# Context products in groups of four slot blocks instead of two, with the value work placed later and the mean loads cut in halves

## The chip, the cores and the metric

The kernel runs on one core of a Trainium2 chip. The time is the device time of one execution in microseconds; the median of three runs of the kernel before is 1081.12 us (1079.87 to 1084.78). Under half a percent, some 5 us, a difference can hardly be told from none.

A core has five engines that run side by side, each with a queue of its own that is worked off in order: TensorE (PE, the matmuls), VectorE (DVE), ScalarE (ACT), GpSimd (POOL, here the indirect DMAs) and SyncE (SP, here all other DMAs). They wait for each other through semaphores. Matmul results land in PSUM, all other tiles lie in SBUF.

## The reference

```python
def _L0_cond_ref(x, mask, Wq, Wo):           # x [16, 512, 1024], mask [16, 1024] of 0 and 1
    xt = jnp.transpose(x, (0, 2, 1))          # [16, 1024 tokens, 512 features]
    q = xt @ Wq.T
    qh = q.reshape(B, T, NH, dk).transpose(0, 2, 1, 3)         # 8 heads of 64
    scores = scale * jnp.einsum('bhqd,bhkd->bhqk', qh, qh)     # queries, keys and values are one
    logits = (scores * cmask + (1.0 - cmask) * NEG) * rmask
    attn = jax.nn.softmax(logits, axis=-1)
    ctx = jnp.einsum('bhqk,bhkd->bhqd', attn, qh)
    return jnp.transpose(ctx... @ Wo.T, (0, 2, 1))
x = x + _L0_cond_ref(x, cond_2048, L0_cond_Wq, L0_cond_Wo)
```

A token whose mask is 0 is no key for the others, and its own row of logits is all zero, so that its attention is the plain mean over all 1024 tokens. About half of the tokens are active.

## The kernel before, in words

**The work of one batch.** There are 16 batches. In each, the active tokens (384 to 544 are allowed for) are given "slots" 0 to 543. `index` makes the list of row numbers, `gather` fetches the rows of x by indirect DMA on POOL (four tiles `xa` of 128 rows and one `xt` of 32), `xt` transposes them on PE (line 424) and `xsplit` splits them into two fp16 halves `xh` (ACT, line 384) and `xl` (DVE, line 385). `query` multiplies them with the weights, three fp16 products for each of 4 feature chunks, so 12 matmuls for one of 8 calls (line 447, copy by ACT in line 450); it is called for e = 0 to 3 (pairs of heads) and g = 0, 1 (halves of the slots). `qsplit` splits the queries again (`hl`, DVE), and four DMAs on SP spread them into a tile `xx` from which the scores are computed. These DMAs are issued one step later than `qsplit` (the list `later`). `value` turns the queries of one pair of heads into rows by slot: 8 small matmuls that read `xx` (line 497), an ACT copy `v` (line 500), squares and maxima on DVE. `peaks`, `top` and `bottom` make from the maxima the shift `nm` for the exponentials. `sum_half` sums the loaded features over the tokens on ACT (line 369), for the mean; `load_all` loads them on SP, 512 KB at a time into one of two `xm` buffers (line 374).

**The steps.** The order of emission is written out in `run`. A batch is a list S of 18 steps: for each pair of heads p = 0 to 3 and each slot block i = 0 to 3 of 128 slots one step, and two more steps (i is None) for the tails of 32 slots (line 595). A step (p, i) emits `scores` for head 2p, then filler work, then `scores` for head 2p+1. One `scores` is 4 matmuls (line 620) into a PSUM tile `pss`, of which there are two, and one exponential on ACT (line 624) from it into a tile `p`, of which there are 9. The context of the step is not computed at once: `attend` is put on the list `todo`. At i = 0 and i = 2 what stands there is moved to `ready`, and at i = 1 and i = 3 it is emitted, so that two slot blocks make one group. A group is the context product of line 643 for two slot blocks: 8 float32 matmuls in the program, each two instructions in the trace, into 64 of the 128 columns of the array, the two heads side by side (`k` is 1, then 0). All of a pair's products add up in one PSUM tile `pav`; `attend` with i = 4 adds the tail (line 647) and copies the sum out on ACT (line 651).

**The filler.** The other work of the batch (`m`) is one list of pairs of a cost and a function: the norms and the projection of the batch before (`project`: 12 matmuls of 512 columns, line 727), the transposes, queries and values of the batch after. `fill` emits from it until the summed cost reaches the share that the list `share` grants for this place. In `m` the letters q, v, P_, x, tc, tv, pk, tp, bt stand for query, value, project, xt, tail_copy, value_tail, peaks, top, bottom; o is the batch before, n the batch after. `free` holds the work of certain steps that costs PE nothing, loads and sums among it. The smaller PSUM tiles of the filler (`pm`) share two buffers, so the next but one waits until the engine that reads a tile has done so.

**What orders the engines.** A scheduler of the framework makes each engine's queue from this order of emission; matmuls of a group are kept together and have a raised priority (`behind`, `high_priority`). The queues themselves are in order: an exponential that has to wait holds back every ACT instruction behind it.

Of the kernel before, what the change touches and what calls it, by code (L numbers as in the profile page):

```python
# [10 lines left out]
F32 = mybir.dt.float32  # L11
# [38 lines left out]
class Fast:  # L50
# [320 lines left out]
    def load_all(self, b, c, after=None):  # L371

        t = self.sb([P, T], F32, "xm", 2)
        self.once(self.nc.sync.dma_start(out=t, in_=self.x_nat[b, c * P:(c + 1) * P, :]), after)
        self.st[b]["xm"].append(t)

    def xsplit(self, dst, src, scaled=False):
# [204 lines left out]
    def scores(self, b, p, i):  # L582
# [6 lines left out]
        if i is None:  # L589
            pt = self.ps_s.tile([P, 2, 512], F32, tag="s", name="pss")  # L590
            for a in range(2):
                for g in range(2):
                    for r in range(HG):
                        xx, k = s["xx"][2 * p + r // 2], r % 2
                        self.beat = nc.tensor.matmul(pt[r * CT:(r + 1) * CT, g, :CH], lhsT=xx[:, 2 * k, 512:C],  # L595
                                                     rhs=xx[:, 2 * k + a, g * CH:(g + 1) * CH],
                                                     start=(a == 0), stop=(a == 1)).ins
            t = self.sb([P, C], F32, "p", 9)
            nc.scalar.activation(t.rearrange("p (g c) -> p g c", g=2), pt[:, :, :CH], AF.Exp,
                                 bias=s["nm"][p][:, HG:], scale=SCALE, accum_out=s["zt"][:, p:p + 1])  # L600

            hi = self.sb([P, C], F32R, "c", 4)
            lo = t.bitcast(F32R)
            nc.vector.tensor_copy(hi, t)
            nc.vector.tensor_tensor(lo, t, hi.bitcast(F32), ALU.subtract)

            def spread():
                s["pt"] = self.sb([P, 2, C], F32R, "pt")
                half = slice(0, DK), slice(DK, P)
                for k in range(2):  # L610
                    nc.sync.dma_start(out=s["pt"][half[k], k, :].bitcast(F32), in_=hi[half[k]].bitcast(F32))
                    nc.sync.dma_start(out=s["pt"][half[1 - k], k, :].bitcast(F32), in_=lo[half[k]].bitcast(F32))

            self.later(spread)
            return None
        xx, k = s["xx"][p // 2], p % 2
        pt = self.ps_s.tile([P, 2, 512], F32, tag="s", name="pss")
        for a in range(2):
            for g in range(2):
                self.beat = nc.tensor.matmul(pt[:, g, :CH], lhsT=xx[:, 2 * k, i * P:(i + 1) * P],  # L620
                                             rhs=xx[:, 2 * k + a, g * CH:(g + 1) * CH],
                                             start=(a == 0), stop=(a == 1)).ins
        t = self.sb([P, C], F32, "p", 9)
        self.exp = [nc.scalar.activation(t.rearrange("p (g c) -> p g c", g=2), pt[:, :, :CH], AF.Exp,  # L624
# [4 lines left out]
    def attend(self, b, p, i, ps):  # L629
        nc, s = self.nc, self.st[b]  # L630

        if i == 1:
            s["pav"] = self.ps_av.tile([P, 2, 512], F32, tag="av", name="pav")
        for g in range(2):
            for k in (1, 0) if i < 4 else range(2):
                cols = slice(g * CH, (g + 1) * CH)
                if i < 4:
                    with ExitStack() as st:
                        if self.group_first:
# [3 lines left out]
                        mm = nc.tensor.matmul(s["pav"][k * DK:(k + 1) * DK, g, :CH], lhsT=s["v"][p][:, i, k * DK:(k + 1) * DK],  # L643
                                              rhs=ps[k][:, cols], start=(i == 1), stop=False)
                    self.group_first = self.group_first or mm.ins
# [199 lines left out]
    def run(self, flag):  # L845
# [99 lines left out]
        if True:  # L945
            for b in range(B + 1):
                o, n = b - 1, b + 1
                if b == B:
                    self.last(o, todo)
                    break  # L950
# [14 lines left out]
                if n < B:  # L965
# [5 lines left out]
                    take = [(0, L(self.gather, b + 2, j)) for j in range(5)] if ahead else []  # L971
                    m = sums + x[:2] + (value(b, 3) if b else []) + pk(b, 1) + second + x[2:4] + rows + x[4:]
                    for g in new[0]:
                        m += [(0, L(self.active, *g))]
                    m += q(0, 0) + tp(b, 1) + (q(0, 1) if b else bt(b, 1) + q(0, 1))
                    for g in new[0]:
# [4 lines left out]
                    for g in new[1]:  # L981
                        m += [(0.1, L(self.facts_end, *g))]
                    m += rng[:2] + tc(0) + tail + v(0) + P_(0) + tv(0) + rest + v(1) + P_(1) + (hot if b else []) + rng[2:] + q(2, 0) + (index if b else [])
                    m += pk(n, 0) + q(2, 1) + tp(n, 0) + P_(2) + (take if b else []) + q(3, 0) + v(2) + bt(n, 0)
                    m += q(3, 1) + tc(1) + [(0, L(self.means, n))] + P_(3) + tv(1)
                    if b == 0:
# [19 lines left out]
                if b + 2 < B:  # L1006
                    self.start(b + 2)
                    for c in range(DC):
                        at = 3 * c + (0 if b else 4)
                        free.setdefault(at, []).append(L(self.load_all, b + 2, c, None if b else first_top))  # L1010
                        free.setdefault(at + 4, []).append(L(self.sum_half, b + 2, c))
                if b == 0:
                    for k in range(2 * DC):
                        free.setdefault(1 + k // 3, []).append(L(self.sum_half, 1, k))

                share = [(1.2, 0) if i is None else ((0.95, 0.95), (0.9, 0), (0.45, 0.95), (0.9, 0))[i] for _, i in S]
                unit = sum(c for c, _ in m) / sum(map(sum, share))
# [10 lines left out]
                for st, (p, i) in enumerate(S):  # L1028
# [15 lines left out]

                    if i in (0, 2):
                        ready, todo = todo, []
                    elif i in (1, 3):
                        self.group_first = None
                        for f in ready[1::-1] + ready[2:]:
                            f()  # L1050
                        ready = []
# [158 lines left out]
```

## Time and profile before

| | |
|---|---|
| median of three runs | 1081.12 us |
| the profiled execution | 1081.4 us, of it a span of 1079.7 us from first to last instruction |
| mean granted clock of TensorE | 0.995 |
| PE busy | 1038.1 us, 96% of the span |
| ACT busy | 681.6 us, 63% |
| DVE busy | 745.6 us, 69% |
| exponentials, line 624 | 512, 717 ns each |
| context products, line 643 | 2048 instructions, busy 262.9 us together |
| scores, line 620 | 2048 instructions, busy 317.6 us together |

A group's line in the profile names the line of the kernel, the engine, the operation, the tiles and shapes, the count, then after a bar the busy time and the mean of one in ns, and after a second bar the time that the engine sat idle just before them and what ended it. In a timeline each row has a start and a length in us, and merges equal instructions; since matmuls are pipelined, lengths of neighbours overlap, and the start of the next row tells when the engine went on.

### The profile page before, as it was taken

To read this page: it belongs to the slowest core of one execution; us is meant where nothing else is said; L and a number is where in the kernel's file an instruction comes from. 1 tells how busy PE (TensorE), PEld (TensorE's weight loads), DVE (VectorE), ACT (ScalarE), POOL (GpSimd) and SP (SyncE) were. 2 spreads that over 40 slices of the span, in tenths; PEclk is the share of its full clock that TensorE was granted. 3 is DMA by queue.
4 is the path that set the end of the run, shared out by engine and by line. 5 is a ranking of instruction groups with operands and counts; after the bars stand their busy time and mean duration, and the time that the engine had idled before them with its cause. 6 is when DMAs were issued, how large, how long until landed. Compare 5 with 4: busy or idle time off the path is not lost.

```text
span 1079.7 us, 23837 instructions
## 1 busy us (share of the span) xinstructions
PE 1038.1 (96%) x8626; PEld 690.9 (64%) x8626; DVE 745.6 (69%) x2376; ACT 681.6 (63%) x1722; POOL 303.0 (28%) x303
## 2 busy tenths in 40 slices
PE   6889999999999999999999999999999999999996
PEld 6566667666666666666666666667666665666553
DVE  6687768676675767766785776868667775666553
ACT  5777667666676766666576666666666565665550
POOL 3101022222202223222233323222232331335652
PEclk9999999999999999999999999999999999999999
DMA  6746465556655554656556566554755554565752
GB/s 205 211 126 177 133 175 154 174 150 190 174 141 158 171 173 145 198 176 169 177 147 197 154 186 193 152 171 135 229 176 173 177 149 127 149 182 166 222 175 84
DMA packets 78125, 181.39 MB, mean 168 GB/s; under 512 B 15008, under 2 KB 16800, under 8 KB 78000
## 3 DMA queue, kind: packets, MB, share of 16 engines
q1 hardware_dynamic: 56816, 111.62, 36.6%
q0 software_dynamic: 21184, 68.18, 20.8%
q8 instruction: 70, 1.15, 0.5%
q14 instruction: 55, 0.45, 0.1%
HBM read 92.34 MB, written 33.91 MB: 117 GB/s over the span
## 4 chain that ended last, share of the span: by engine, by line
PE 82%; DMA 7%; DVE 3%; ACT 2%; issue 2%; SPq 2%; POOL 0%; POOLq 0%; ACTq 0%; DVEq 0%
PE pav L643 21%; PE pss L620 19%; PE pm L727 15%; PE pm L447 14%; DMA xx<-hl 6%; PE pm L424 3%; PE pav L647 3%; PE pss L595 2%; PE pm L497 2%; PE pm L680 1%; ACT q L450 1%; SPq L470 1%; ACT p L624 1%; PE pm L520 1%; DMA rb<-rd 1%
## 5 line engine op out<-in xcount | busy, mean ns | idle before, releaser
L624 ACT ACTIVATE p<-pss,nm 128x544 f32<-128x544 f32 x512 | 365.5, 717 | 210.5 <-PE pss L620 203.6
L620 PE MATMUL pss<-xx 128*128 128x272 f16 x2048 | 317.6, 280 | 3.1 <-ACT p L624 2.7
L643 PE MATMUL pav<-p,v 128*64 128x272 f32 x2048 | 262.9, 399 | 0.0
L620 PEld LDWEIGHTS <-xx 128*128 128x128 f16 x2048 | 191.9, 100 | 73.2 <-issue 27.7
L643 PEld LDWEIGHTS pav<-p,v 128*64 128x64 f32 x2048 | 135.6, 136 | 94.3 <-issue 27.1
L811 POOL DMA_INDIRECT y_out<-xa,idx x68 | 70.2, 1032 | 288.6 <-issue 91.5
L447 PE MATMUL pm<-xh,wqh 128*128 128x274 f16 (+1 forms) x512 | 143.3, 280 | 3.3 <-DVE nm L560 1.9
L447 PE MATMUL pm<-xl,wqh 128*128 128x274 f16 (+1 forms) x512 | 142.9, 279 | 0.2 <-DVE xl L385 0.2
L447 PE MATMUL pm<-xh,wql 128*128 128x274 f16 (+1 forms) x512 | 143.0, 279 | 0.0
L339 POOL DMA_INDIRECT xa<-x_in,idx x68 | 69.5, 1023 | 167.1 <-PE pss L620 71.0
L447 PEld LDWEIGHTS <-wqh 128*128 128x128 f16 x1024 | 99.3, 98 | 25.9 <-issue 6.7
L811 POOL DMA_INDIRECT y_out<-xi,idx x60 | 74.0, 1233 | 137.7 <-DVE xi L798 38.3
L624 ACT ACTIVATION_READ_ACCUMULATOR p<-pss,nm 128x1 f32 x512 | 102.6, 200 | 0.0
L450 ACT ACTIVATE q<-pm 128x272 f32<-128x272 f32 (+1 forms) x128 | 50.8, 397 | 81.6 <-PE pm L447 81.6
L727 PE MATMUL pm<-woh,ch 128*128 128x512 f16 x240 | 91.8, 382 | 0.3 <-DVE tmp L523 0.3
L727 PE MATMUL pm<-wol,ch 128*128 128x512 f16 x240 | 91.7, 382 | 0.0
L727 PE MATMUL pm<-woh,cl 128*128 128x512 f16 x240 | 91.5, 381 | 0.0
L732 DVE SCALAR_TENSOR_TENSOR xa<-pm,xa 128x512 f32<-128x512 f32 x60 | 41.4, 690 | 72.4 <-PE pm L727 72.3
L339 POOL DMA_INDIRECT xi<-x_in,idx x60 | 61.3, 1021 | 106.1 <-PE pss L620 49.5
L727 PEld LDWEIGHTS <-ch 128*128 128x128 f16 x480 | 46.7, 98 | 45.6 <-issue 2.2
L369 ACT ACTIVATE xm<-xm 128x1024 f32<-128x1024 f32 (+1 forms) x62 | 62.5, 1009 | 2.3 <-DMA xm<-x_nat_in 2.3
L711 DVE TENSOR_TENSOR c<-c,rb 128x544 f32<-128x544 f32 x64 | 46.1, 720 | 22.4 <-PE pss L620 11.1
(194 smaller groups left out, 1550.0 us busy)
## 6 DMA issues: line engine op xcount, KB each, us to landing
xx<-hl SPq DMA_DIRECT2D x256, 136.0 KB
xm<-x_nat_in SPq DMA_DIRECT2D x56, 512.0 KB
rb<-rd SPq DMA_DIRECT2D x128, 136.0 KB
pt<-c SPq DMA_DIRECT2D x64, 136.0 KB
pt<-p SPq DMA_DIRECT2D x64, 136.0 KB
ub<-ud SPq DMA_DIRECT2D x16, 256.0 KB
xi<-x_nat_in SPq DMA_DIRECT2D x8, 256.0 KB
xa<-x_in,idx POOLq DMA_INDIRECT x68, 4.5
```

Source lines behind the costliest of these rows:

```text
L339: dma = self.nc.gpsimd.indirect_dma_start(out=tile[:n], out_offset=None, in_=self.x, in_offset=bass.IndirectOffsetOnAxis(ap=idx, axis=0))
L369: self.nc.scalar.activation(s["xm"][k], s["xm"][k], AF.Copy, accum_out=s["ms2"][:, k:k + 1])
L424: self.pe = nc.tensor.transpose(pt[:, c, :], x[:n, c * P:(c + 1) * P], self.ident[:n, :n]).ins
L447: self.beat = nc.tensor.matmul(pq, lhsT=w[:, c, e * P:(e + 1) * P], rhs=xx[:, c, cols], start=(k == 0), stop=(k == 3 * DC - 1)).ins
L450: nc.scalar.activation(s["q"][:, e, cols], pq, AF.Copy, scale=1.0 / (SX * SW))
L620: self.beat = nc.tensor.matmul(pt[:, g, :CH], lhsT=xx[:, 2 * k, i * P:(i + 1) * P], rhs=xx[:, 2 * k + a, g * CH:(g + 1) * CH], start=(a == ...
L624: self.exp = [nc.scalar.activation(t.rearrange("p (g c) -> p g c", g=2), pt[:, :, :CH], AF.Exp, bias=s["nm"][p // HG][:, p % HG:p % HG + 1 ...
L643: mm = nc.tensor.matmul(s["pav"][k * DK:(k + 1) * DK, g, :CH], lhsT=s["v"][p][:, i, k * DK:(k + 1) * DK], rhs=ps[k][:, cols], start=(i == ...
L711: self.once(nc.vector.tensor_tensor(c, c, s["rb"][p], ALU.mult), self.beat if p < 3 else None)
L727: nc.tensor.matmul(po[:cols.stop - cols.start], lhsT=a[:, e, cols], rhs=w[:, e, :], start=(e == 0 and k == 0), stop=(e == DC - 1 and k == 2))
L732: self.nc.vector.scalar_tensor_tensor(x, po, 1.0 / (SX * SW), x, ALU.mult, ALU.add)
L811: dma = self.nc.gpsimd.indirect_dma_start(out=self.out, out_offset=bass.IndirectOffsetOnAxis(ap=idx, axis=0), in_=x, in_offset=None)
```

## The change

The context groups become twice as long: `ready` is filled at i = 0 alone and emitted at i = 1, all four slot blocks of the pair of heads before, in the order 3, 2, 1, 0 (and then the tail, where it is there). There are 12 buffers for `p` instead of 9. In `m`, each `value` stands further behind, the peaks of the later heads as well, and the grants in `share` differ. `load_all` becomes two DMAs of 256 KB, the second one a step after the first, and the sum comes three steps after the first half instead of four.

```diff
     def load_all(self, b, c, after=None):
         t = self.sb([P, T], F32, "xm", 2)
-        self.once(self.nc.sync.dma_start(out=t, in_=self.x_nat[b, c * P:(c + 1) * P, :]), after)
+        self.load_part(t, b, c, 0, after)
         self.st[b]["xm"].append(t)
+
+    def load_part(self, t, b, c, k, after=None):
+        cols = slice(k * T // 2, (k + 1) * T // 2)
+        self.once(self.nc.sync.dma_start(out=t[:, cols], in_=self.x_nat[b, c * P:(c + 1) * P, cols]), after)
...
-        t = self.sb([P, C], F32, "p", 9)
+        t = self.sb([P, C], F32, "p", 12)
...
-        if i == 1:
+        if i == 3:
             s["pav"] = self.ps_av.tile([P, 2, 512], F32, tag="av", name="pav")
...
-                                              rhs=ps[k][:, cols], start=(i == 1), stop=False)
+                                              rhs=ps[k][:, cols], start=(i == 3), stop=False)
...
-                    self.last(o, todo)
+                    self.last(o, todo[3::-1] + todo[4:])
...
-                    m = sums + x[:2] + (value(b, 3) if b else []) + pk(b, 1) + second + x[2:4] + rows + x[4:]
+                    m = sums + x[:2] + second + x[2:4] + (value(b, 3) if b else []) + rows + x[4:] + pk(b, 1)
...
-                    m += q(0, 0) + tp(b, 1) + (q(0, 1) if b else bt(b, 1) + q(0, 1))
+                    m += q(0, 0) + (q(0, 1) + tp(b, 1) if b else tp(b, 1) + bt(b, 1) + q(0, 1))
...
-                    m += rng[:2] + tc(0) + tail + v(0) + P_(0) + tv(0) + rest + v(1) + P_(1) + (hot if b else []) + rng[2:] + q(2, 0) + (index if b else [])
-                    m += pk(n, 0) + q(2, 1) + tp(n, 0) + P_(2) + (take if b else []) + q(3, 0) + v(2) + bt(n, 0)
-                    m += q(3, 1) + tc(1) + [(0, L(self.means, n))] + P_(3) + tv(1)
+                    m += rng[:2] + tc(0) + tail + P_(0) + v(0) + tv(0) + rest + P_(1) + (hot if b else []) + rng[2:] + q(2, 0) + v(1) + (index if b else [])
+                    m += q(2, 1) + pk(n, 0) + P_(2) + (take if b else []) + tp(n, 0) + q(3, 0) + bt(n, 0)
+                    m += q(3, 1) + v(2) + tc(1) + [(0, L(self.means, n))] + P_(3) + tv(1)
...
-                        free.setdefault(at + 4, []).append(L(self.sum_half, b + 2, c))
+                        free.setdefault(at + 1, []).append(lambda n=b + 2, c=c: self.load_part(self.st[n]["xm"][c], n, c, 1))
+                        free.setdefault(at + 3, []).append(L(self.sum_half, b + 2, c))
...
-                share = [(1.2, 0) if i is None else ((0.95, 0.95), (0.9, 0), (0.45, 0.95), (0.9, 0))[i] for _, i in S]
+                share = [(1.2, 0) if i is None else ((1.0, 0.6), (0.1, 0.5), (0.9, 1.0), (0.9, 0.9))[i] for _, i in S]
...
-                    if i in (0, 2):
+                    if i == 0:
                         ready, todo = todo, []
-                    elif i in (1, 3):
+                    elif i == 1:
                         self.group_first = None
-                        for f in ready[1::-1] + ready[2:]:
+                        for f in ready[3::-1] + ready[4:]:
                             f()
```

More of the change, by code (lines that the diff above doesn't have):

```diff
@@ L622, in scores @@
                                              start=(a == 0), stop=(a == 1)).ins
-        t = self.sb([P, C], F32, "p", 9)
+        t = self.sb([P, C], F32, "p", 12)
         self.exp = [nc.scalar.activation(t.rearrange("p (g c) -> p g c", g=2), pt[:, :, :CH], AF.Exp,
```

## The prediction

> **What bounds the kernel now.** First the busy times, the slices and the chain of the page.
>
> ```profile
> PE 1038.1 (96%) x8626; PEld 690.9 (64%) x8626; DVE 745.6 (69%) x2376; ACT 681.6 (63%) x1722; POOL 303.0 (28%) x303
> PE   6889999999999999999999999999999999999996
> PEclk9999999999999999999999999999999999999999
> PE 82%; DMA 7%; DVE 3%; ACT 2%; issue 2%; SPq 2%; POOL 0%; POOLq 0%; ACTq 0%; DVEq 0%
> ```
>
> PE is full from slice 4 on, at a clock that no change can raise, and 82% of the chain is PE. So only two things give time: fewer microseconds of PE work, or fewer gaps in it. For the work I looked at the context group around 508 us in the PE timeline, in windows so narrow that rows are not merged.
>
> ```profile
> 507.99 0.28 PE L620 MATMUL pss<-xx 128*128 128x272 f16 x1
> 508.20 0.45 PE L643 MATMUL pav<-p,v 128*64 128x272 f32 x2
> ...
> 509.62 0.40 PE L643 MATMUL pav<-p,v 128*64 128x272 f32 x2
> 509.85 0.40 PE L643 MATMUL pav<-p,v 128*64 128x272 f32 x2
> ...
> 510.18 0.33 PE L680 MATMUL pm<-ident,rcol 128*128 128x128 f32 x1
> ```
>
> Pairs of context matmuls (two heads side by side) follow each other every 0.23 us. But the first starts 0.21 us after the last score, where scores follow each other after 0.116, and the next work starts 0.33 us after the last pair instead of 0.23: about 0.1 us lost going in and 0.1 coming out. The trace's starts give 0.05 more between the first pair and the second (0.28). So a group carries 0.247 us beside its work, and there are 4 x 2 x 16 = 128 groups.
>
> For the gaps I read the waits of PE and a place where they stand.
>
> ```profile
> L497 PE MATMUL pm<-two,xx 128*128 128x64 f16 x480 | 26.6, 193 | 13.1 <-DMA xx<-hl 11.4 <-ACT qt L508 1.3
> L620 PE MATMUL pss<-xx 128*128 128x272 f16 x2048 | 317.6, 280 | 3.1 <-ACT p L624 2.7 <-DMA xx<-hl 0.2
> ```
>
> ```profile
> 503.32 0.19 PE L497 MATMUL pm<-two,xx 128*128 128x64 f16 x1 [1.32 <-ACT qt L508]
> ...
> 505.27 0.38 PE L497 MATMUL pm<-two,xx 128*128 128x64 f16 x7 [0.86 <-DMA xx<-hl]
> ```
>
> The value matmuls are the one group that PE stands still for: 13.1 us, nearly all for the spread of the queries that has not landed. Scores wait 3.1 us for the exponentials in the whole run, so ACT is no bound.
>
> **The change, part by part.** The sum is made against the profiled execution, 1081.4 us, which is 0.3 us above the median of 1081.12.
>
> *Groups of four.* The instructions are the same 2048. The built program's order shows 64 unbroken groups of 16 program matmuls where there were 128 of 8, so 64 entries and exits go: 64 x 0.247 = 15.8 us, all on PE and so on the path. A rule here: the Trainium skill (TensorEngine Tiling (Array Packing), Tiling Modes) says that a change of tiling mode drains the array, and its page TensorE: Matmul & The Clock Gate (Single matmul latency) puts the fixed part of a lone warm matmul at some 166 ns. An estimate from that page, a full drain in and one out, is 64 x 2 x 0.166 = 21 us. The row's 0.1 us each way is this shape itself, so I take 15.8.
>
> *Later values.* In the built order `value` 0 and 1 each have a projection (12 x 0.215 = 2.6 us) or more put ahead of them, `value` 2 a query (12 x 0.116 = 1.4 us) and more. The longest wait for the spread is 1.9 us, so 2.6 us cover it. The last batch keeps its order; its two waits, 0.65 and 0.93 us, stay. That is 13.1 - 1.6 = 11.5; I take 11.0. What is late next is the maxima, the shift and the attends of the same pair, and those come a step or more later.
>
> *Fewer groups starve and crowd ACT.* In a group of 16 x 0.23 + 0.25 = 3.9 us ACT gets no scores; it has at most two exponentials left over and the splits. It issues one per 0.69 us:
>
> ```profile
> 484.92 0.72 ACT L624 ACTIVATE p<-pss,nm 128x544 f32<-128x544 f32 x1
> 485.52 0.22 ACT L624 ACTIVATION_READ_ACCUMULATOR p<-pss,nm 128x1 f32 x1
> 485.61 0.73 ACT L624 ACTIVATE p<-pss,nm 128x544 f32<-128x544 f32 x1
> ```
>
> Per pair of heads ACT needs 8 x 0.69 = 5.5 us for them and some 3.5 for the rest, PE about 16. Outside the group that is 7.6 us in 12, which fits on average; the crowd is at the batch boundary. I worked out its order from the built program, T = 0 at the end of the first group of a batch. PE: eight transposes to 0.87, two scores to 1.8, the tail's products to 2.3, value 3 to 2.55, tail scores to 3.15, a transpose to 3.3, one score to 3.8, then the transposes of `xt`, which need the buffer of value 3. ACT in its order: two splits `xh` (0.49 each) to 1.6, two exponentials to 3.0, the copy `c` to 3.5, the copy `v` to 4.0, its data to 4.1. So `xt` waits 0.35 us; in the variant of the order where it follows the tail scores directly, 0.8. I take 0.5 x 14 boundaries = 7 us. The matmul of `bottom` now follows the transpose of `top` by one score and a bit (0.58 us), while VectorE needs until about 0.8: 0.24 x 14 = 3.4 us. At its old place `bottom` made queries wait for 1.9 us in all; that goes, -1.9.
>
> *12 buffers for p.* Live at the group are 8 of the pair before, one tail and up to 4 new ones, 13. But the built order puts the group ahead of the last of these scores, so that its exponential waits for a group that PE has finished anyway: nothing. Were it not so, one exponential of two groups per batch would wait some 3 us, with ACT idle in that time.
>
> *Start and end.* In the first batch ten score blocks run before any context product can fill in for waiting on exponentials and sums; I put 1 us. In the last batch there is little filler, and now three scores follow each other ahead of a group at three or four places; the third waits 0.67 (from the start of a score to its exponential) + 0.72 - 0.93 = 0.46 us each: 2 us.
>
> *Halved loads.* 56 more DMAs on SP, 0.36 us to issue each, 20 us of a queue that mostly waits; what they pass are the spreads, later by 0.36. [...] In the trace a 512 KB load has all its packets done 2.5 to 5.6 us after its issue. The shortest distance in the built order from the second half to its sum is 51 PE matmuls, some 7 us. So I take 0. If cover were gone, ACT would stand in front of the sum and the exponentials behind it: 56 times what is missing. The sum itself (1.04 us) moves from a place beside a group into the crowd at the boundary; its cost is from 0 to 0.3 x 14 = 4 us, and since ACT catches up in the next query, I take 0. POOL's gathers keep their places to within a filler item and are waited for by nobody on PE now.
>
> Sum: -15.8 - 11.0 - 1.9 + 7.0 + 3.4 + 1 + 2 = -15.3; 1081.4 - 15.3 = 1066.
>
> **The rivals.**
>
> *Everything is hidden.* ACT and VectorE orders are looser than I read, the boundary costs nothing: -15.8 - 11 - 1.9 = 1052.7. For it: ACT is busy 63%. Against: the two PSUM buffers `pm` tie `xt` to the copy `v` in the built order.
>
> *Waits only move.* The value wait goes, but each batch pays all bounds at once (0.8 + 0.24 + 0.3 for the sum, and another 0.5 in the copies now that the tail's products and a value stand next to each other): 1.85 x 14 = 26 us. Then the group's saving alone is left, with the start and end against it: 1081.4 - 15.8 - 12.9 + 26 + 3 = 1082, no change. For it: `c` and `v` copies now queue behind each other three times a batch.
>
> *Slower: ACT starvation.* Each group empties ACT for about 2.5 us, and if the scores after it then wait for one exponential (0.72 us) in each of 64 groups, that is +46: 1081.4 - 28.7 + 46 + 3 = 1102. It decides from 0.4 us per group (28.7 - 3 over 64). Against it: the 3.1 us of such waits now, and that both `pss` are free after a group.
>
> *The change doesn't do what it says.* The queue could break the groups up; the built order has them whole, so only a saving per group smaller than 0.247 is left. At half, 1074.
>
> **How the numbers follow.** Forecast as summed, 1060 to 1073: 0.50. Everything hidden, down to 1052: 0.18. Waits only move or half the saving, 1073 to 1086: 0.22. Starvation, over 1086: 0.10. Half a percent is 5.4 us, about what a measurement of this kernel can tell from no change: faster is below 1075.7. It takes the first two and 0.07 of the third, 0.75; the same 0.14; slower 0.11. The range from 1054 to 1082 leaves out the tip of the hidden case and the starved one.
>
> **What would show it.** Context matmuls: the next work starts 0.33 us after the last pair, but only 64 times; busy time of line 643 falls by the 64 x 0.247. The idle time before the value matmuls falls from 13.1 to about 2 us. Idle time before the transposes of `xt`, ended by the copy `v`, comes up by several us; scores wait for exponentials for 5 us or less. The sums' wait for their loads stays near 2.3 us. The forecast is wrong if scores wait for exponentials for over 20 us in total, if sums wait for loads by more than 10, or if the first batch is longer by more than 4.

## The result, and the profile after

The changed kernel takes 1067.91 us (median of 4 runs, 1066.27 to 1070.45). The kernel before, run beside it, takes 1081.39 us (median of 4). The ratio is 0.988, with a 95% interval from 0.986 to 0.990, so the change takes 13 us away (here and below, differences in us are worked out from the ratios; the medians alone would give up to 1.6 us more or less). The profiled execution took 1066.27 us with a span of 1064.6 us; that of before had a span of 1079.7 us. The difference of the spans is 15.1 us.

First the busy times and the chain on the page of the changed kernel:

```profile
PE 1021.8 (96%) x8626; PEld 701.2 (66%) x8626; DVE 730.2 (69%) x2376; ACT 670.1 (63%) x1722; POOL 296.8 (28%) x303
...
PE 75%; ACT 8%; DVE 8%; issue 4%; DMA 3%; POOL 0%; SPq 0%; POOLq 0%; DVEq 0%; ACTq 0%
```

PE does the same 8626 matmuls in 16.3 us less busy time, at the same mean clock (0.994, before 0.995). On the chain its share fell from 82% to 75%, DMA's from 7% to 3%; ACT and DVE rose from 2% and 3% to 8% each. So PE has less to do, and on this chain ACT and DVE hold it up more often. From the groups of the changed kernel, with the idle time behind the second bar:

```profile
L624 PE MATMUL pss<-xx 128*128 128x272 f16 x2048 | 305.8, 279 | 4.6 <-ACT p L628 3.7
L647 PE MATMUL pav<-p,v 128*64 128x272 f32 x2048 | 248.8, 396 | 0.0
...
L501 PE MATMUL pm<-two,xx 128*128 128x64 f16 x480 | 24.5, 194 | 1.0 <-DMA xx<-hl 1.0
```

Lines above 372 have moved by 4. The context matmuls (line 643 before, 647 now) went from 262.9 to 248.8 us busy, the values (497, now 501) from 13.1 us of idle time to 1.0. PE's waits (place, what it waited for, us in total, times, the longest):

```profile
PE pm L684 <- DVE rcol L678: 7.0, 10, 0.7
PE pm L451 <- DVE xa L736: 4.9, 5, 1.2
PE pss L624 <- ACT p L628: 3.7, 10, 0.4
...
PE pm L562 <- DVE m L555: 1.4, 5, 0.6
...
PE pm L428 <- ACT v L504: 0.2, 1, 0.2
```

Line 684 is `recip_rows`, the transpose of the reciprocal sums, which waited for nothing before. `bottom` (562) and `xt` (428) are the waits that the prediction priced at the batch boundary; the first two rows are not in it. Here are three places in the timeline. First a group of four:

```profile
304.80 0.63 PE L624 MATMUL pss<-xx 128*128 128x272 f16 x4
305.36 0.68 PE L647 MATMUL pav<-p,v 128*64 128x272 f32 x4
...
308.62 0.63 PE L647 MATMUL pav<-p,v 128*64 128x272 f32 x4
309.18 0.41 PE L624 MATMUL pss<-xx 128*128 128x272 f16 x2
```

From the first context matmul to the next score there are 3.82 us, in one piece. By the trace's starts the group is entered 0.209 us after the last score and left 0.325 us after its last pair (medians). Both are the same as before, but come 64 times instead of 128. Second, the three scores in a row of which the last waits:

```profile
299.19 0.63 PE L624 MATMUL pss<-xx 128*128 128x272 f16 x4
...
299.76 0.63 PE L624 MATMUL pss<-xx 128*128 128x272 f16 x4
299.85 0.72 ACT L628 ACTIVATE p<-pss,nm 128x544 f32<-128x544 f32 x1
300.56 0.70 ACT L628 ACTIVATE p<-pss,nm 128x544 f32<-128x544 f32 x1
300.71 0.28 PE L624 MATMUL pss<-xx 128*128 128x272 f16 x1 [0.32 <-ACT p L628]
```

There are two `pss`; the third score needs the first of them, which is free when the exponential of 299.85 has read it. And third, the transpose of `recip_rows` and the chain on DVE that it waits for:

```profile
525.59 0.72 DVE L609 TENSOR_TENSOR p<-p,c 128x544 fp32r<-128x544 f32 x1
...
526.36 0.28 PE L562 MATMUL pm<-ident,m 128*128 128x4 f32 x2
526.43 0.31 DVE L675 TENSOR_TENSOR rcol<-zt,corr 32x1 f32<-32x1 f32 x2
526.78 0.22 DVE L677 RECIPROCAL rcol<-rcol 128x10 f32<-128x10 f32 x1
527.03 0.17 DVE L678 TENSOR_TENSOR rcol<-rcol,hit 128x10 f32<-128x10 f32 x1
...
527.34 0.30 PE L684 MATMUL pm<-ident,rcol 128*128 128x128 f32 x1 [0.70 <-DVE rcol L678]
```

DVE has a 0.72 us split of a tail (line 609) in the middle of the small steps that make `rcol`, and PE, which has nothing before the transpose but two tiny matmuls, stands for 0.70 us.

The idle time of the page counts only from the modelled end of a matmul. To compare whole kernels I also took the distance from the start of one matmul to the start of the next, less the distance that the same pair of lines takes at its quick tenth in all profiles, and added what is over by more than 0.06 us. This is called standing time below. Stretches of 3.4 or 6.8 us in which TensorE had half its clock are left out of it; every profile has a few, not always in the same places, and so kernels are compared by ratios on the same chip and not by single spans. A wait that falls into such a stretch is left out with it. That happens above all in the first 90 us, so the last row gives the same count without them (here stands under 0.13 us between matmuls of one line are left out). With this last rule for the whole run, the rows of the table change by up to 2 us and the sums of all profiles by up to 4, so smaller differences should not be read. Standing time in us, by the work that came next:

| | before | after | groups only | old shares | rows later |
|---|---|---|---|---|---|
| values (501) | 15.6 | 1.4 | 18.2 | 10.7 | 1.9 |
| scores (624) | 6.5 | 12.0 | 25.2 | 26.0 | 12.3 |
| queries (451) | 6.5 | 8.9 | 2.8 | 9.8 | 9.7 |
| recip_rows (684) | 0.0 | 8.5 | 1.4 | 0.1 | 1.3 |
| bottom (562) | 0.1 | 3.6 | 1.2 | 2.8 | 3.5 |
| xt (428) | 6.7 | 3.1 | 5.9 | 2.7 | 5.0 |
| everything | 39.5 | 45.1 | 62.7 | 58.3 | 39.1 |
| everything behind 90 us | 26.7 | 36.0 | 51.6 | 48.7 | 29.9 |

(The last three kernels are experiments.) The row of `xt` misleads: 3.4 of its 6.7 us are the wait for the first gather of the run, which the changed kernel has too (3.1 us from start to start at 11.4 us), but under a stretch of half clock. Behind 90 us `xt` stands for 2.0 us before and 2.8 after. So the changed kernel stands more than the one before, by 5.6 us, or 9.3 behind the first 90. It is faster although it waits more, because its work is shorter: 64 groups less, at 0.247 us each, are 15.8 us.

### The profile page after: what moved, and what is told of

It reads as the page before. It is cut to its first block, busy times and chain, and to the rows that moved or that the text cites. A ratio compares the mean times of both kernels' runs of the same rounds, so it can differ in the third digit from the quotient of the medians.

```text
span 1064.6 us, 23887 instructions
## 1 busy us (share of the span) xinstructions
PE 1021.8 (96%) x8626; PEld 701.2 (66%) x8626; DVE 730.2 (69%) x2376; ACT 670.1 (63%) x1722; POOL 296.8 (28%) x303
## 4 chain that ended last, share of the span: by engine, by line
PE 75%; ACT 8%; DVE 8%; issue 4%; DMA 3%; POOL 0%; SPq 0%; POOLq 0%; DVEq 0%; ACTq 0%
PE pav L647 22%; PE pss L624 17%; PE pm L731 15%; PE pm L451 13%; ACT p L628 4%; PE pm L428 2%; PE pav L651 2%; ACT xh L388 2%; DVE p L609 1%; DMA xx<-hl 1%; ACT v L504 1%; PE pm L501 1%; PE pm L684 1%; ACT p L603 1%; DVE rcol L675 1%
## 5 line engine op out<-in xcount | busy, mean ns | idle before, releaser
L624 PE MATMUL pss<-xx 128*128 128x272 f16 x2048 | 305.8, 279 | 4.6 <-ACT p L628 3.7
L647 PE MATMUL pav<-p,v 128*64 128x272 f32 x2048 | 248.8, 396 | 0.0
L647 PEld LDWEIGHTS pav<-p,v 128*64 128x64 f32 x2048 | 141.3, 137 | 91.1 <-issue 13.9
L815 POOL DMA_INDIRECT y_out<-xa,idx x68 | 73.1, 1076 | 299.5 <-PE pss L624 147.5
L628 ACT ACTIVATION_READ_ACCUMULATOR p<-pss,nm 128x1 f32 x512 | 105.3, 206 | 0.0
L815 POOL DMA_INDIRECT y_out<-xi,idx x60 | 67.4, 1124 | 105.4 <-PE pss L624 48.9
L802 DVE TENSOR_TENSOR xi<-xi,ub 128x512 f32<-128x512 f32 (+1 forms) x60 | 40.7, 688 | 43.2 <-PE pss L624 40.9
L715 DVE TENSOR_TENSOR c<-c,rb 128x544 f32<-128x544 f32 x64 | 46.2, 722 | 31.1 <-PE pm L451 19.4
```

The costliest lines, as they stand in the source:

```text
L715: self.once(nc.vector.tensor_tensor(c, c, s["rb"][p], ALU.mult), self.beat if p < 3 else None)
L802: self.once(self.nc.vector.tensor_tensor(x[:n], x[:n], s["ub"][:n], ALU.add), self.beat)
L815: dma = self.nc.gpsimd.indirect_dma_start(out=self.out, out_offset=bass.IndirectOffsetOnAxis(ap=idx, axis=0), in_=x, in_offset=None)
```

## The experiments

Each ratio is to the kernel before, run beside it on the same chip. Its median there was 1086.3 us for the first four kernels, 1085.67 for the next four and 1081.56 for the last four. The diffs show the lines that matter; `...` and lines not shown stand for the rest of an edit.

### Groups of four alone

The kernel before with groups of four and 12 buffers for `p`; its list, shares and loads stay. (The start of `pav` moves with the order, as in the change.)

```diff
-                    if i in (0, 2):
+                    if i == 0:
                         ready, todo = todo, []
-                    elif i in (1, 3):
+                    elif i == 1:
                         self.group_first = None
-                        for f in ready[1::-1] + ready[2:]:
+                        for f in ready[3::-1] + ready[4:]:
```

> The kernel before with groups of four slot blocks and 12 buffers for p alone; old list of filler, old shares, whole loads. Theory (a group costs 0.247 us beside its work): 64 groups fewer take 15.8 us off PE, the value waits of 13 us stay, start and end give back about 3: 1081.4 - 13 = 1068. Rival (the gain is the later values, and the group's edges were hidden under other waits): within 4 us of before, 1077 to 1085. Rival (ACT runs dry during long groups): slower than before, scores wait over 20 us for exponentials.

1090.21 us, ratio 1.0036 (1.0009 to 1.0064): slower, where 1068 was expected. Its waits of PE:

```profile
PE pm L497 <- DMA xx<-hl: 17.0, 17, 2.9
PE pss L620 <- ACT p L624: 4.2, 9, 1.5
```

The 64 groups are there, entered after 0.209 us and left after 0.325, and the busy time of the context is 250.5 us. The 15.8 us are saved on PE. But the values wait 17.0 us for the spread instead of 11.4, at 17 places and up to 2.9 us, and by the standing time scores went from 6.5 to 25.2. Together the standing time grows by 23.2 us. 23.2 - 15.8 = +7.4; measured +3.9, and +8.0 for the profiled execution, which at 1094.3 us was slower than the median. A saving of work on PE is no saving of time here as long as the other work keeps its place. It fits that the group that is missing at i = 3 was the cover under which the spread landed and the exponentials were worked off. For the exponentials the runs on the shares below test it; for the spread no run does, since all later ones have the new list.

### The later values alone

The kernel before with the new list `m`.

```diff
-                    m = sums + x[:2] + (value(b, 3) if b else []) + pk(b, 1) + second + x[2:4] + rows + x[4:]
+                    m = sums + x[:2] + second + x[2:4] + (value(b, 3) if b else []) + rows + x[4:] + pk(b, 1)
...
-                    m += rng[:2] + tc(0) + tail + v(0) + P_(0) + tv(0) + rest + v(1) + P_(1) + ...
+                    m += rng[:2] + tc(0) + tail + P_(0) + v(0) + tv(0) + rest + P_(1) + ... + q(2, 0) + v(1) + ...
```

> The kernel before with the new list of filler alone (later values, later peaks); groups of two, old shares, whole loads. Theory: the value matmuls' wait falls from 13.1 to about 2 us and nothing else moves, 1081.4 - 11 = 1070. Rival (the waits only move to the transposes of xt, the shift or the next queries): the value wait falls all the same, but the time stays within 4 us of before, 1077 to 1085.

1080.15 us, ratio 0.9936 (0.9909 to 0.9962), so -7.0 us. Its waits of PE:

```profile
PE pm L497 <- DMA xx<-hl: 1.2, 2, 0.9
```

The wait for the spread went from 11.4 to 1.2, as priced. By the standing time the values give 15.6 - 6.3 = 9.3 us back and the scores take 3.5 of it (6.5 to 10.0); in all it falls from 39.5 to 32.0, by 7.5. Part of the wait moved. The queries' wait for `project` (DVE, `xa`) appears here already, with 1.9 us at 5 places. Behind the first 90 us the values give 12.2 us back and everything together only 2.5, with 4.8 more at the scores.

### The halved loads alone

```diff
-        self.once(self.nc.sync.dma_start(out=t, in_=self.x_nat[b, c * P:(c + 1) * P, :]), after)
+        self.load_part(t, b, c, 0, after)
...
-                        free.setdefault(at + 4, []).append(L(self.sum_half, b + 2, c))
+                        free.setdefault(at + 1, []).append(lambda n=b + 2, c=c: self.load_part(self.st[n]["xm"][c], n, c, 1))
+                        free.setdefault(at + 3, []).append(L(self.sum_half, b + 2, c))
```

> The kernel before with the loads in two halves and the sums a step sooner alone. Theory: hidden, within 2 us of before, sums wait for their loads for less than 5 us. Rival (a fixed price of each DMA, or sums that hold the exponentials back): 56 more transfers cost 5 us or more, and the wait of the sums or of the scores rises by as much.

1081.15 us, ratio 0.9943 (0.9921 to 0.9965): -6.2 us, where nothing was expected. What changes on DVE is its wait for the sums. Before:

```profile
DVE ms L434 <- ACT xm L369: 10.1, 14, 1.5
```

With the halved loads:

```profile
DVE ms L438 <- ACT xm L369: 2.0, 6, 0.4
```

DVE stood for a sum once a batch, 14 times, and that has nearly gone. A late start of a query by 0.25 us in 12 batches went too, and the standing time of queries fell from 6.5 to 3.1. But this is not shown to come from DVE's wait: the edit also changed the built order of PE. In 12 batches four score matmuls instead of two now stand between the transpose of `top` and the next query. In the kernel before, that query starts only when ACT has copied the query ahead of it out of a `pm` buffer (in one batch the last score starts at 301.05 us, the copy ends at 301.37, the query starts at 301.42), and the two further scores fill this time. Groups only and groups of one lose these late starts as well (queries 2.8 and 2.3 us), while DVE stands there before the sums about as long as in the kernel before (8.7 and 8.6 us, for most of which the profile names nothing). The late starts make some 3 of the 6.2 us. The standing time of all falls from 39.5 to 32.5, but behind the first 90 us only by 1.9, so the rest stays open. Loads and sums moved together here; that the sum comes a step sooner, which the prediction had put at 0 to 4 us of loss, is no loss in this order.

### Groups of one

The kernel before with every slot block on its own, so that there are 254 groups; list, shares and loads stay. (`pav` starts at i = 0; once a batch the tail's products come with a slot block.)

```diff
-                    if i in (0, 2):
-                        ready, todo = todo, []
-                    elif i in (1, 3):
+                    if i is not None and len(todo) > 1:
                         self.group_first = None
-                        for f in ready[1::-1] + ready[2:]:
-                            f()
+                        todo.pop(0)()
```

> The kernel before with every slot block a context group of its own, one step later than its scores; 254 groups in place of 128, the same matmuls. Theory: 126 x 0.247 = 31 us more, 1112; the starts show 0.21 into each group and 0.33 out of it. Rival (the edges are hidden or the cost is not per group): under 8 us more. Rival (evenly spread groups feed ACT better): faster than before.

1121.28 us, ratio 1.032 (1.0274 to 1.0367), +34.8 us where +31 was expected. Context matmuls in the groups of the profile, and its largest wait of PE:

```profile
L643 PE MATMUL pav<-p,v 128*64 128x272 f32 x2048 | 291.4, 406 | 2.6 <-ACT c L651 2.6
...
PE pm L680 <- DVE nm L560: 14.4, 13, 1.6
```

The same 2048 instructions are busy for 291.4 us instead of 262.9. Entry and exit are 0.209 and 0.325 us again. The standing time grew by 5.9 us to 45.4, so (34.8 - 5.9) / 126 = 0.23 us per extra group, close to the 0.247 read from the starts (from the profiled spans, with the clock taken off as in the account below, 0.26). With 64, 128 and 254 groups entry and exit are the same. The new wait is at `recip_rows`, with the old list and shares, but not for `rcol`: the profile names `nm`, the step on DVE that empties the `pm` buffer of `bottom` and that stands behind three steps of `norm`. Where the transpose starts at 286.54 us, after 1.33 us of idle time, `rcol` had been ready for 1.7 us and `nm` for 0.1.

### The whole change with groups of two

```diff
-                    if i == 0:
+                    if i in (0, 2):
                         ready, todo = todo, []
-                    elif i == 1:
+                    elif i in (1, 3):
                         self.group_first = None
-                        for f in ready[3::-1] + ready[4:]:
+                        for f in ready[1::-1] + ready[2:]:
```

> The changed kernel with groups of two again (and the buffers for p left at 12); new filler, new shares, halved loads stay. Theory (a group's edges cost 0.247 us wherever they stand): 15.8 us over the changed kernel or more, ratio to before 1.000 to 1.006, 128 groups with 0.21 in and 0.33 out. Rival (the gain is the filler, the shares and the loads): ratio below 0.993.

1088.03 us, ratio 1.0018 (0.9995 to 1.0040): the gain is gone. Its waits of PE:

```profile
PE pm L684 <- ACT p L628: 6.5, 9, 0.7
```

The edges are back, and the wait of `recip_rows` stays. The row names ACT, but the timeline shows the same wait as in the changed kernel: in one place DVE ends `rcol` at 288.64 us, and the transpose starts at 288.79.

### The whole change with the old shares

```diff
-                share = [(1.2, 0) if i is None else ((1.0, 0.6), (0.1, 0.5), (0.9, 1.0), (0.9, 0.9))[i] for _, i in S]
+                share = [(1.2, 0) if i is None else ((0.95, 0.95), (0.9, 0), (0.45, 0.95), (0.9, 0))[i] for _, i in S]
```

> The changed kernel with the old shares; groups of four, new filler, halved loads stay. Theory (longer groups open waits of the scores for exponentials that only the new shares close): 8 us or more over the changed kernel, ratio 0.995 or more, and scores, transposes and queries stand still for 8 us more in total. Rival (the shares do nothing by themselves): ratio 0.985 to 0.991, as the whole change.

1086.39 us, ratio 0.9992 (0.9972 to 1.0012): the gain is gone here too. Its waits of PE:

```profile
PE pss L624 <- ACT p L628: 7.5, 22, 1.4
PE pm L451 <- DVE xa L736: 5.4, 5, 1.2
```

The old shares grant nothing behind the second score at i = 1 and i = 3, where a group of two used to stand. With groups of four there is none at i = 3: the scores of two steps follow each other directly, and scores wait for an exponential at 22 places; they stand for 26.0 us instead of 12.0. The wait of `recip_rows` is not in it (0.1 us of standing time): the wait for `rcol` belongs to the new shares, as it is there in the run before as well, with groups of two.

### The whole change with whole loads

The load and the sum of the kernel before, all else as changed.

```diff
-                        free.setdefault(at + 1, []).append(lambda n=b + 2, c=c: self.load_part(self.st[n]["xm"][c], n, c, 1))
-                        free.setdefault(at + 3, []).append(L(self.sum_half, b + 2, c))
+                        free.setdefault(at + 4, []).append(L(self.sum_half, b + 2, c))
```

> The changed kernel with whole loads and sums four steps after the load. Theory (sums a step sooner take away VectorE's wait for the last sum, some 10 us in its queue, and with it 0.25 us of PE per batch): 4 to 6 us over the changed kernel, ratio 0.991 to 0.994, and VectorE waits for the sums again for 5 us or more. Rival (nothing is behind that wait once the filler is new): ratio as the whole change, 0.986 to 0.990.

1070.64 us, ratio 0.9855 (0.9819 to 0.9891). The whole change has 0.9879 on its own chip, so the halved loads bring nothing in it. DVE's wait for the sums with whole loads and all else changed:

```profile
DVE ms L434 <- ACT xm L369: 1.9, 3, 0.7
```

So the rest of the change takes away what the halved loads took away alone. The new list by itself does not: in the run with the later values alone this wait is 5.7 us at 7 places, and 2.6 at 3 more for which the profile names nothing. Neither the 6 us nor the 56 further DMAs are found in the time.

### Value 3 behind the transposes

The prediction had put 7 us on a buffer that value 3 hands to the transposes of `xt`. So value 3 goes behind them.

```diff
-                    m = sums + x[:2] + second + x[2:4] + (value(b, 3) if b else []) + rows + x[4:] + pk(b, 1)
+                    m = sums + x[:2] + second + x[2:4] + rows + x[4:] + (value(b, 3) if b else []) + pk(b, 1)
```

> The changed kernel with value 3 of the running batch put behind the transposes of xt. Theory (the transposes of xt wait 0.31 us for the copy of value 3 at most boundaries, because both share two PSUM buffers): that wait goes, 2 to 4 us under the changed kernel, ratio 0.984 to 0.987. Rival (the wait moves to the next query, which then needs the same buffer): ratio 0.987 to 0.990, unchanged.

1078.68 us, ratio 0.9939 (0.9915 to 0.9963): about 6 us worse than the changed kernel. Its waits of PE:

```profile
PE pm L562 <- DVE m L555: 4.8, 10, 0.7
PE pss L624 <- ACT p L628: 4.7, 4, 3.0
```

The stand of `xt` falls from 3.1 to 1.0 us, but the maxima of value 3 now come later, and `bottom`, which transposes them, stands for 8.2 us instead of 3.6; everything together 54.0 instead of 45.1, with one wait of 3.0 us of a score in the last batch.

### Values and loads, without groups and shares

The new list and the halved loads in the kernel before: groups of two, old shares (the two diffs of groups of two and old shares above, both made to the changed kernel; the 12 buffers stay).

> The kernel before with the later values and the halved loads together: groups of two and the old shares are kept (127 groups). Theory, that the single gains overlap because both take out waits of the same queries and maxima, and that the whole change's 13 us need the long groups: ratio to before 0.991 to 0.995, the wait of the values near 1 us, the wait of VectorE for the sums near 2 us as with the new list alone. Rival, that the single gains add up: 0.9936 x 0.9943 = 0.988, as fast as the whole change, and then the groups of four add nothing to the rest of it.

1075.86 us, ratio 0.9953 (0.9932 to 0.9975): -5.1 us. The gains of -7.0 and -6.2 do not add up. The two waits are small, as expected: values wait 1.0 us for the spread, DVE 0.9 for the sums. With this run there is a square of four kernels, all with the new list, the halved loads and 12 buffers:

| us against before | old shares | new shares |
|---|---|---|
| groups of two | -5.1 | +2.0 |
| groups of four | -0.9 | -13.1 |

Each has an interval of about 2 us to either side. With the new shares the long groups give 15.1 us, nearly the whole 15.8 of their edges; with the old shares they cost 4.2 us. And the new shares by themselves cost 7.1. Neither does any good without the other. The new shares with the old list were not tried: there a value would be read before its spread has been issued.

### The changed kernel once more

Unchanged, on the chip of the last four kernels.

> The changed kernel once more, so that the others of this call have it on their own chip. Expected 0.986 to 0.990 of before. All theories agree here.

1069.07 us, 1067.29 to 1070.47 in four runs; ratio 0.9888 (0.9849 to 0.9926).

### recip_rows a step later

`recip_rows` is put in a fixed step for p = 0 to 2 only (for p = 3 it stands in `m`), so the edit moves it for the third pair of heads alone. That is the place where it waits.

```diff
-                            free.setdefault(st + 3, []).append(L(self.recip_rows, b, p))
+                            free.setdefault(st + (3 if p < 2 else 4), []).append(L(self.recip_rows, b, p))
```

> The changed kernel with the transposes of the reciprocal sums (recip_rows) one step later for the third and fourth pair of heads. In the changed kernel TensorE stands still for about 7 us in 10 places before these transposes, since the column of reciprocals from VectorE is not there yet. Theory, that this wait is on the path: it goes, and the kernel takes 3 to 6 us less than the changed one, 0.982 to 0.985 of before. Rival, that what is not waited for here is waited for a little later (the work behind it on VectorE is late in the same way, as in the groups of four put into the old order): within 2 us of the changed kernel, and the wait shows up at the queries or the scores.

1061.2 us, 1060.26 to 1063.51 in four runs; ratio 0.9814 (0.9775 to 0.9853). That is 7.9 us less than the changed kernel beside it, whose fastest run is 1067.29. Its waits of PE:

```profile
PE pm L451 <- DVE xa L736: 4.9, 5, 1.2
...
PE pss L624 <- ACT p L628: 4.0, 11, 0.5
...
PE pm L684 <- DVE xl L389: 0.2, 1, 0.2
```

The 7.0 us of `recip_rows` became 0.2, the other rows are as in the changed kernel, and nothing took the place of the wait. Beside the second profile of the changed kernel, from the same chip, `recip_rows` gives 7.3 us of standing time back and all together 8.1 (47.2 to 39.1). So this wait was on the path.

### recip_rows later, whole loads

The edit of the run before and the loads of the kernel before.

> The changed kernel with the transposes of the reciprocal sums later, as in the run before, and with whole loads of 512 KB and sums four steps after them, as in the kernel before. Theory, that the loads no longer matter once the list is new: the same as the run before to 0.3%. Rival, that the halved loads' earlier sums matter for VectorE's order at the place of the transposes: slower than the run before by 3 us or more.

1060.35 us, 1058.86 to 1061.00; ratio 0.9805 (0.9768 to 0.9841): the same as the run before within what can be told. This is the best version: groups of four, the new list and shares, `recip_rows` of the third pair a step later, and the loads left whole. It beats the changed kernel by some 9 us and the kernel before by some 21.

### The account of all of them

The change of standing time, 0.247 us less or more for each group, and half the length of the half-clock stretches (the end of the run left out), all from the profiles and against the kernel before (39.5 us standing, 128 groups, 3.4 us lost to stretches), beside the change of the profiled span (before 1079.7):

| kernel | groups | standing | edges | half clock | sum | span |
|---|---|---|---|---|---|---|
| changed kernel | 64 | +5.6 | -15.8 | 0 | -10.2 | -15.1 |
| the same, second profile | 64 | +7.7 | -15.8 | -1.7 | -9.8 | -14.2 |
| groups only | 64 | +23.2 | -15.8 | +5.1 | +12.5 | +12.8 |
| values only | 128 | -7.5 | 0 | +5.1 | -2.4 | -1.4 |
| loads only | 128 | -7.0 | 0 | +5.1 | -1.9 | -0.5 |
| groups of one | 254 | +5.9 | +31.1 | +1.7 | +38.7 | +40.1 |
| whole change, groups of two | 127 | +3.3 | -0.2 | +8.5 | +11.6 | +7.9 |
| whole change, old shares | 64 | +18.8 | -15.8 | +3.4 | +6.4 | +5.4 |
| whole change, whole loads | 64 | +9.6 | -15.8 | +1.7 | -4.5 | -12.2 |
| value 3 later | 64 | +14.5 | -15.8 | 0 | -1.3 | -4.7 |
| values and loads | 128 | -3.3 | 0 | -1.7 | -5.0 | -8.4 |
| rows later | 64 | -0.4 | -15.8 | 0 | -16.2 | -20.1 |
| rows later, whole loads | 64 | -4.1 | -15.8 | 0 | -19.9 | -22.6 |

The edits of one part, groups of one and the old shares come out within 1.4 us. The other kernels are faster than the sum by 3 to 5 us, the one with whole loads by 7.7. The standing time is known to some 4 us only, and in the first 90 us waits and half clock cover each other, so differences of this size cannot be read one by one. A part of what is left is in seams between other kinds of work, which are in no column: outside the context groups the changed kernel's PE goes from one line to another 984 times, before 1057 times, and counted with the quick tenths of all distances that is some 2 to 3 us. The rest was not found.

## Why the prediction was right, and where its steps were not

The time was predicted as 1066 us and measured as 1067.91; the change of the sum was -15.3 and the measured one -13.1. Its two large terms hold, and of the small ones most do not. The terms beside the groups were to add up to +0.5. By the standing time values (-14.2), scores (+5.5), queries (+2.4), `recip_rows` (+8.5), `bottom` (+3.5) and `xt` (+0.8, behind 90 us) make +6.5, and the kernel is some 5 us faster than that account. That the total came within 2 us is partly luck.

**Groups of four, -15.8: right, and the best supported term.** Entry and exit are the same in all kernels, line 647 fell by 14.1 us of busy time, and groups of one cost 0.23 us each. The rule that was weighed against it, a full drain and refill at a lone matmul's fixed 166 ns each way (the Trainium skill, TensorEngine Tiling (Array Packing), Tiling Modes, and TensorE: Matmul & The Clock Gate, Single matmul latency), gives an estimate of 0.33 us per group, or 42 us for the 126 groups that groups of one add; 28.9 were measured behind the waits. The row was the better source. That the groups use 64 of the 128 columns, and not that they are float32, goes with the price: the tail's float32 product over all 128 columns (651) starts 0.028 us after the last score (median), the fp16 scores of the tail in 32 columns (599) 0.209 after it, like a group (50 cases in all profiles). What the prediction did not say is the condition: alone this edit makes the kernel 3.9 us slower, and it pays only with the new shares (15.1 us against 4.2 lost). Of its sentence on ACT, that the work "fits on average; the crowd is at the batch boundary", the second half holds only in part: with the new shares a third score in a row waits for an exponential at six places in the middle of the run, and with the old ones scores stand for 25 to 26 us.

**Later values, -11.0: right in its wait.** 13.1 us became 1.0 on the page; of the last batch's two waits of 1.6 us, which were expected to stay, none did, and the 1.0 left is one early wait at 95 us. Alone, the edit gave 7.0 us, since scores and the matmul of `bottom` behind the moved values began to wait.

**The batch boundary, +7.0 for `xt`: wrong.** The named wait, for the copy `v`, is 0.2 us on the page. By the starts `xt` stands for 0.31 us at eight boundaries, 2.5 us, where the kernel before has 0.14 at fourteen, 2.0: a loss of less than 1 us and not of 7. The order was read right, the delay of ACT was taken too long, and at the other boundaries nothing waits. **`bottom`, +3.4: right** (3.6 us of standing time, 0.1 before), though spread unevenly, with 0.38 us at four boundaries and 0.14 or nothing at most others.

**Queries, -1.9: wrong in sign.** The wait for `bottom` went, but in five batches a query waits up to 1.2 us for `project` on DVE (line 736), 4.9 us in all; standing time went from 6.5 to 8.9. This wait comes with the new list: it is 0.8 to 2.2 us with whole loads or with groups of two, and 4.9 to 5.4 where halved loads and groups of four are both there. Why the two together double it was not found.

**`recip_rows`, not in the sum: +8.5.** This is the largest thing that the prediction missed. It looked at each moved item and at the boundary, but not at what comes in a fixed step (`free`) when the filler in front of it changes. Only the new shares bring this wait for `rcol`, by the runs with groups of two and with old shares (in groups of one the same transpose waits for another thing, a `pm` buffer), and moving it a step gave 7.9 us.

**Start and end, +1 and +2: the end right, the middle missed, the start not seen.** In the last batch three scores in a row stand at three places, 0.59 us each (at 986.47, 999.73 and 1012.06 us), 1.8 us for the 2 that were priced; that the last batch is only 0.1 us worse in all is mostly because its two value waits went. What the prediction missed is the same thing in the middle of the run, 0.48 us at six places; in all scores stand for 5.5 us more (6.5 to 12.0). For the start no loss is seen: the first 90 us stand for 8.3 us, 10.0 in the second profile of the same kernel, and 13.4 before, where 3.4 are the first gather.

**Halved loads, 0: right for the whole change, and wrong alone.** In the changed kernel they cost and bring nothing (0.9855 without them, 0.9879 with). In the old order the halved loads with the sooner sum took 8 of DVE's 10.1 us of waiting away, changed PE's order beside `top`, and brought 6.2 us. **12 buffers, 0:** no run here separates them from the groups.

**The rivals.** Everything hidden (1052.7) is refuted by 5.6 us more of standing time instead of some 13 less; a later `recip_rows` reaches 1060 to 1061 us. Waits only move is the truth of the groups alone and of the old shares, and not of the whole. Starvation of ACT (0.4 us per group) did not come: scores wait 3.7 us for exponentials. Half the saving per group is excluded by the starts and by groups of one.

## What to carry to other kernels

Work that is taken off the engine that bounds a kernel can have been cover for another engine or a DMA. Here the saving was worth its full price only with the filler spread anew, and each of the two alone lost; so price a regrouping together with the shares that fill the gaps. An edit to loads can also change the built order of another engine's queue, so compare the orders before giving a gain a cause. List not only the moved items but everything that sits in a fixed step near them, and check on which engine its input is made and what is queued ahead of it there. Read the waits of the result again: a new wait of 0.7 us in 10 places was worth 7.9 us for a change of one line.

## What the runs showed that was not expected

- The cost of entering and leaving a group of 64-column float32 matmuls is constant: 0.209 us from the last score's start and 0.325 us from the last pair's start, with 64, 128 and 254 groups.
- Gains of single edits do not add up: -7.0 and -6.2 us alone, -5.1 together; +3.9 us for groups alone, -13.1 with the rest.
- 112 loads of 256 KB instead of 56 of 512 KB on SP made no difference that these runs can tell with the rest of the change, in two pairs of kernels (0.9879 against 0.9855, 0.9814 against 0.9805).
- A long stand of PE was often followed by a stretch at half clock. These are stretches of the kernel before, a row each: from and to in us, length, busy time and instructions by engine (PE first), then TensorE's granted clock (PEclk column), the DMA share and GB/s.

```profile
880.00:889.00 9.00, 8.91 (x77) 6.60 (x76) 6.42 (x24) 6.02 (x16) 2.89 (x3) 1.00 0.84 185
889.00:894.00 5.00, 1.94 (x20) 1.04 (x18) 3.52 (x13) 2.42 (x6) 1.23 (x1) 1.00 1.00 252
894.00:897.40 3.40, 3.40 (x9) 1.21 (x8) 0.69 (x1) 1.22 (x2) 0.00 (x0) 0.50 0.73 166
```

At 889 us two values stand for the spread, 2.2 and 1.5 us from start to start, and then the clock is 0.50 for 3.4 us, which costs another 1.7. Between 90 and 1050 us all 14 profiles together have 8 such stretches. Each begins within 3 us of the end of a stand of 1.9 us or more (from start to start); four other stands of 2.0 to 3.2 us had none behind them, and none comes after shorter stands alone. This was seen, not tested.
